# A graph-attention and hypergraph kernel: first two pairs laid out anew, half a weights' sum off TensorE, node degrees of two pairs by one-column products, two leaky heads moved behind an eviction

## The chip, the cores and the metric

One NeuronCore of one Trainium2 chip runs the whole program. The metric is the device time of one execution in microseconds. Three executions of the kernel before took 2388.04, 2384.32 and 2381.41 us; their median, 2384.32 us, is what a change is held against.

## The reference, cut to what matters

There are 128 graphs of 128 nodes with 512 features, and a 128x128 adjacency matrix for each. Layer 0 is graph attention with eight heads, layer 1 a hypergraph network with a hidden width of 1024; each ends in a residual and a layer norm.

```python
# layer 0
feats = einsum('bnf,hfu->bhnu', X, W)                  # 8 heads of 64
dense = leaky_relu(e_self[..., :, None] + e_neigh[..., None, :], 0.2)
att   = softmax(dense + NEG_BIG * (1 - A))
x = layernorm(x + relu(einsum('bhij,bhju->bhiu', att, feats) + b))
# layer 1: H = (adj != 0), w = first row of adj
Dn = einsum('nce,ne->nc', H, w);  Dn = where(Dn > 0, 1/Dn, 0)
Be = H.sum(axis=1);               Be = where(Be > 0, 1/Be, 0)
conv(x, W) = Dn * (H @ (Be * (H.T @ (x @ W.T)))) + b   # used twice
x = layernorm(x + conv(layer_norm(relu(conv(x, W1))), W2) + x)
```

All arithmetic is float32. The biases are zero and the norms' gains one in the data, but the kernel reads them.

## The kernel before, in words

The graphs are taken two at a time, as 64 pairs. The work of a pair runs over about five periods, so that in any one period several pairs are under way, each in another stage ("lag"). The order of the work is written out by hand: every step has a time on a scale with a period of T = 38.6, all steps are sorted by it, and the instructions are issued in that order on the engine that each step names. The numbers are thus keys for an order and no measured times. The dictionary `first` gives single steps of early pairs a key of their own. Each engine takes its instructions strictly in that order, as does the queue of SP, which issues nearly all transfers.

In one period TensorE does, for the pairs then due: `propagate` (tile `pz`: y times the propagator R), `propagator` (`pd`), the hidden layer's chain (`phX`, `phY`, `phW`), `output` (`pq`), the chain of the features (`pfX`, `pfY`, `pfW`), the attention products (`pav`), and the chain of the second layer (`pyX`, `pyY`, `pyW`). Each chain computes a 2x2 blocked product with seven block products instead of eight (a Winograd form). It needs sums of blocks of the data (`zS`, `xS`, `hS`, made by GpSimd, here POOL) and of the weights (made once). In a chain the accumulator `X` is copied out by ScalarE (`ph`, `pf`, `py`, line 359) between two of its products, and the next product into the same bank waits for the copy. PSUM has eight banks, given out in turn.

Steps that the change and the prediction touch:

- `prepare_hidden` (L249) makes sums of W1's blocks on POOL. The sum called s3 is made on TensorE instead, by `prepare_hidden_products` (L263, L264): the identity times one block minus the identity times another, in two halves of 512 columns, each evicted by ScalarE (`prepare_hidden_out`, L267).
- `nodes` (L375 to L384) computes 1/Dn: VectorE multiplies the mask by the first row, which has been spread over all partitions by DMA (`load_first_row`, two transfers of 64 KB), sums along the row, inverts, transposes. `write_nodes` sends it to DRAM, `spread_nodes` brings it back on all partitions as `dnb`. `r_evict` (L468) multiplies `pd` by it.
- Attention scores of a pair come as rows in DRAM (`spread_rows`: DVE `rows`, L559, then the transfer `rd`), are spread to all partitions (`neighbours`: the transfer `nb`), masked on POOL (`masked`, L608, four instructions of four heads), put through leaky ReLU on ScalarE (`leaky`, L624, one instruction for each head, four for each g and q), reduced by VectorE (`largest`, L630), exponentiated on ScalarE (`exponential`, L638), sent to DRAM (`e_write`, `ed`) and read back in blocks (`e_read`, `eb`) for VectorE's 32x32 transpose (`eT`, L659).
- `z_evict` (L866) is ScalarE's copy of `pz`; the first product of the hidden chain waits for it. On ScalarE it stands behind `leaky(0, 0)` and `leaky(0, 1)` of a later pair. `z_sums` (L877) on POOL follow, behind the four mask instructions.
- `relu` (L918), `square` (L929), `y_sum` (L972), `skip` (L842) and `f_sum` (L526) belong to the chains' ends.

Of the kernel before, what the change touches and what calls it, by code (L numbers as in the profile page):

```python
# [8 lines left out]
F32 = mybir.dt.float32  # L9
AF = mybir.ActivationFunctionType  # L10
ALU = mybir.AluOpType
# [9 lines left out]
def kernel(  # L21
# [45 lines left out]
    nc = tc.nc  # L67
    G, N, F = x.shape
    P = 128
# [3 lines left out]
    KF = F // P  # L73
# [3 lines left out]
    HH = H // 2  # L77
# [11 lines left out]
    def bank(name):  # L89
        return psum.tile([P, HALF], F32, tag="bank", name=name)  # L90
# [17 lines left out]
    def load_first_row(p):  # L108
        s = st[p]
        s["w"] = work.tile([P, 2, N], F32, tag="w", name=f"w_{p}", bufs=2)  # L110
        for g in range(2):
            nc.sync.dma_start(s["w"][:, g, :], adj[2 * p + g, 0, :].partition_broadcast(P))
# [92 lines left out]
    ident = const.tile([P, P], F32, name="ident")  # L205
# [52 lines left out]
    def prepare_hidden_banks():  # L258
        made["s3"] = [bank(f"s3_{k}") for k in range(KF // 2)]

    def prepare_hidden_products():
        for k, t in enumerate(made["s3"]):
            nc.tensor.matmul(t, ident, w1_sb[:, 0, k, :], start=True, stop=False)  # L263
            nc.tensor.matmul(t, made["minus"], w1_21[:, k, :], start=False, stop=True)  # L264

    def prepare_hidden_out(k):
        nc.scalar.copy(w1_sb[:, 5, k, :], made["s3"][k])  # L267

# [99 lines left out]
    @step(0, 11.0)  # L368
    def nodes(p, s):

        a = s["a"]
        dd = small.tile([P, 2], F32, tag="dd", name=f"dd_{p}")
        w = s["w"]
        for g in range(2):
            nc.vector.scalar_tensor_tensor(  # L375
                w[:, g, :], a[:, g, :], 0.0, w[:, g, :], op0=ALU.not_equal, op1=ALU.mult,
                accum_out=dd[:, g:g + 1],
            )
        t = dn[:, :2]
        nc.vector.tensor_scalar(t, dd, TINY, None, op0=ALU.max)  # L380
        nc.vector.reciprocal(t, t)
        nc.vector.scalar_tensor_tensor(t, dd, 0.0, t, op0=ALU.is_gt, op1=ALU.mult)
        s["dr"] = work.tile([P, B], F32, tag="dr", name=f"dr_{p}")
        nc.vector.transpose(s["dr"], dn)  # L384

    @step(0, 17.0)
# [224 lines left out]

    def leaky(p, s, g, q):
        if (p, g, q) == (0, 1, 1):

            hs = slice(HH, H)
            t = s["nb"][:, g, HH * N:].rearrange("p (h j) -> p h j", h=HH)
            nc.vector.tensor_tensor(
                t, t, s["ft"][:, g, hs, 0:1].to_broadcast([P, HH, N]), op=ALU.add
            )
            nc.vector.scalar_tensor_tensor(t, t, SLOPE, t, op0=ALU.mult, op1=ALU.max)  # L620
            return
        for h in range(q * HH, (q + 1) * HH):
            t = scores(p, s, g, h)
            nc.scalar.activation(t, t, AF.Prelu, bias=s["ft"][:, g, h, 0:1], alpha=SLOPE)  # L624
# [534 lines left out]
    for t, fn, *args in (  # L1159
# [25 lines left out]
        (78.985, prepare_hidden_banks, ()), (98.05, prepare_hidden_products, ()),  # L1185
        (116.95, prepare_hidden_out, (0,)), (119.86, prepare_hidden_out, (1,)),
        (15.5, prepare_output_vectors, ()), (16.0, prepare_output, ()),
        (78.3, prepare_rows, ()), (78.79, prepare_output_sums, ()),
        (78.99, prepare_output_spread, (0, "gw")), (98.0, prepare_output_spread, (1, "bw")),
        (98.1, prepare_output_bias, ()), (98.2, prepare_output_blocks, (slice(0, 1),)),  # L1190
        (98.25, prepare_output_blocks, (slice(1, 2),)),
# [8 lines left out]

    first = {
        ("square", 0, 0, 1): 134.82,
        ("square", 0, 0, 0): 134.81,
        ("scale_edges", 2): 139.25,
        ("exponential", 1, 1, 0): 126.51,
        ("squares", 0, 1, 2): 144.2,
# [3 lines left out]
        ("first_output", 0, 0): 97.817,  # L1210
        ("write_nodes", 2): 147.1,
        ("nodes", 2): 147.0,
        ("edges", 3): 149.9,
# [5 lines left out]
        
        ("scale_edges", 1): 119.84,  # L1220
        ("edges", 1): 98.5,
        ("exponential", 1, 1, 1): 126.52,
        
        ("exponential", 1, 0, 1): 121.77,
        ("exponential", 1, 0, 0): 119.9,
        ("largest", 1, 1, 1): 121.9,
        ("largest", 1, 1, 0): 119.83,
        ("largest", 1, 0, 1): 117.83,
        ("largest", 1, 0, 0): 98.3,
        ("leaky", 1, 1, 1): 121.8,  # L1230
        ("leaky", 1, 1, 0): 119.82,
# [13 lines left out]
        
        ("propagator", 1): 121.7, ("spread_nodes", 1): 80.3, ("r_evict", 1): 121.8,
        ("leaky", 0, 1, 1): 77.65, ("leaky", 0, 0, 1): 73.6, ("largest", 0, 0, 1): 75.3,
# [13 lines left out]
        
        ("nodes", 3): 154.6, ("write_nodes", 3): 154.7, ("skip", 0): 132.5,
    }
# [4 lines left out]
    for p, time, fn, *args in (  # L1268
# [5 lines left out]
        (1, 15.6, plain_features_out), (1, 97.9, adj_transpose_first),  # L1274
        (0, 78.8, e_transpose_first, 0, 0), (0, 78.85, e_transpose_first, 0, 1),
        (0, 97.815, rstd_first, 0), (0, 97.816, shift_first, 0),
        (0, 97.835, rstd_first, 1), (0, 110.32, shift_first, 1),
# [3 lines left out]
    for p in range(PAIRS):  # L1281
# [4 lines left out]
        for lag, time, name, pairs, fn, args in steps:  # L1286
            if p not in pairs:
                continue
            if p == 0 and lag == 2 and time < 8.5:
                time *= 0.2  # L1290
            if p == LAST:

# [64 lines left out]
```

## Time and profile before

| | |
|---|---|
| three executions | 2388.04, 2384.32, 2381.41 us; median 2384.32 us |
| the profiled execution | 2381.18 us, its span 2379.4 us |
| TensorE busy (matmuls) | 2358.8 us, 99% of the span |
| weight loads, VectorE, POOL, ScalarE busy | 78%, 87%, 77%, 64% |
| granted TensorE clock, mean | 0.999 |
| DMA | 347.09 MB, mean 146 GB/s |

The profile is of one execution; 1.8 us of its time lie outside its span. The page gives busy shares of engines over the whole span. Since one engine is nearly always busy, the time is read from the few places where that engine stands idle. The timeline lists the instructions in order with the idle time ahead of each in square brackets, and what ended it. A start of one group less the start of the group before is the time that the first really takes; the printed durations overlap by some 0.15 us. The waits list who waited for whom in total. PE is TensorE, DVE is VectorE, ACT is ScalarE.

### The profile page before, as it was taken

The page shows a single profiled execution, that of the slowest core. Times are in us where ns is not written, and L with a number is a line of the kernel's source. Part 1 is how long each engine was busy: PE and PEld are TensorE (multiplying, and loading weights), DVE is VectorE, ACT ScalarE, POOL GpSimd, SP SyncE. Part 2 cuts the span into 40 slices and gives each one's busy share as a digit, 9 for nine tenths or more (in the row PEclk, how much of TensorE's full clock was granted, in tenths as well). Part 3 has the DMA queues.
Part 4 walks back from the last instruction along what each step waited for, and adds up shares of the span by engine and source line. Part 5 has one row for each costly group of instructions (what it writes and reads, how often), then busy time and mean ns, then how long its engine had stood idle before and what let it go on. Part 6 is the DMA issues. An engine that isn't in the chain of part 4 may idle for free.

```text
span 2379.4 us, 80693 instructions
## 1 busy us (share of the span) xinstructions
PE 2358.8 (99%) x32317; PEld 1867.3 (78%) x32317; DVE 2077.1 (87%) x4451; ACT 1530.4 (64%) x4489; POOL 1826.4 (77%) x2062
## 2 busy tenths in 40 slices
PE   8999999999999999999999999999999999999998
PEld 6788887887877878778778778788787787787886
DVE  7988988889889898898898898988988988889886
ACT  5676675666766756667667667566676676665663
POOL 5878777787787777877877877778778778787784
PEclk9999999999999999999999999999999999999999
DMA  7555455545544555455555545554555455455431
GB/s 203 142 159 144 141 157 143 151 141 150 151 143 143 155 147 147 146 149 148 150 144 156 143 143 155 150 144 145 149 149 148 147 147 151 141 157 143 146 118 50
DMA packets 431134, 347.09 MB, mean 146 GB/s; under 512 B 151440, under 2 KB 380328, under 8 KB 430760
## 3 DMA queue, kind: packets, MB, share of 16 engines
q1 hardware_dynamic: 427288, 337.46, 49.7%
q8 instruction: 256, 4.19, 0.7%
q10 hardware_dynamic: 3472, 4.47, 0.6%
q14 instruction: 118, 0.97, 0.2%
HBM read 239.08 MB, written 102.73 MB: 144 GB/s over the span
## 4 chain that ended last, share of the span: by engine, by line
PE 93%; DMA 3%; POOL 1%; ACT 1%; DVE 1%; issue 1%; SPq 0%; ACTq 0%; POOLq 0%; DVEq 0%
PE phX L97 18%; PE pyX L97 17%; PE pfX L97 9%; PE phW L97 9%; PE pyW L97 9%; PE pfW L97 4%; PE phY L97 4%; PE pav L724 4%; PE pq L97 4%; PE pz L97 4%; PE pyY L97 4%; PE pfY L97 2%; PE pd L97 1%; DMA nb<-rd 1%; DMA ed<-nb 1%
## 5 line engine op out<-in xcount | busy, mean ns | idle before, releaser
L359 ACT COPY py<-pyX 128x257 f32<-128x257 f32 x189 | 70.6, 374 | 526.4 <-PE pyX L97 458.9
L97 PEld LDWEIGHTS phX<-zS,w_sb 128*64 128x64 f32 x6144 | 345.3, 137 | 35.9 <-POOL ft L763 23.7
L97 PE MATMUL phX<-zS,w_sb 128*64 128x128 f32 x6144 | 368.0, 273 | 0.7 <-POOL xS L486 0.7
L941 POOL TENSOR_TENSOR sq<-sq 128x512 f32<-128x512 f32 (+2 forms) x384 | 343.8, 896 | 20.0
L608 POOL TENSOR_TENSOR nb<-nb,neg 128x512 f32<-128x512 f32 x256 | 319.6, 1282 | 35.2 <-DMA nb<-rd 34.8
L624 ACT ACTIVATE nb<-nb,ft 128x128 f32<-128x128 f32 x1020 | 325.4, 392 | 19.7 <-POOL nb L608 19.5
L638 ACT ACTIVATE nb<-nb,nm 128x128 f32<-128x128 f32 x1024 | 319.1, 392 | 0.2 <-DVE nm L630 0.2
L788 POOL TENSOR_TENSOR rso<-veo,mhalf 128x2 f32<-128x2 f32 x63 | 44.1, 700 | 337.5 <-DVE veo L786 337.5
L918 ACT ACTIVATE h<-h,vecs 128x128 f32<-128x128 f32 x768 | 240.0, 393 | 1.9 <-DVE h L903 1.4
L97 PE MATMUL pyW<-w_sb,hS 128*64 128x256 f32 x2016 | 239.5, 379 | 1.2 <-DVE y L972 1.2
L97 PE MATMUL pyX<-w_sb,h 128*64 128x257 f32 x2016 | 240.1, 379 | 0.5 <-ACT py L359 0.5
L97 PE MATMUL pyX<-w_sb,hS 128*64 128x257 f32 x2016 | 240.2, 379 | 0.1
L630 DVE TENSOR_REDUCE nm<-nb 128x4 f32<-128x512 f32 x256 | 175.2, 684 | 55.9 <-ACT nb L624 45.1
L763 POOL TENSOR_TENSOR ft<-ft,b_bc 128x512 f32<-128x512 f32 x128 | 204.5, 1617 | 5.0 <-ACT ft L550 5.0
L97 PEld LDWEIGHTS pyX<-w_sb,h 128*64 128x64 f32 x2016 | 144.8, 136 | 75.1 <-ACT py L359 0.9
L97 PEld LDWEIGHTS pyW<-w_sb,hS 128*64 128x64 f32 x2016 | 143.9, 136 | 75.7 <-DVE y L972 1.6
L97 PEld LDWEIGHTS pyX<-w_sb,hS 128*64 128x64 f32 x2016 | 138.9, 136 | 65.4 <-POOL hS L486 0.2
L659 DVE STREAM_TRANSPOSE eT<-eb 128x512 f32<-128x512 f32 x252 | 163.4, 685 | 3.3 <-DMA eb<-ed 2.4
L842 DVE SCALAR_TENSOR_TENSOR o<-y,b_bc 128x512 f32<-128x512 f32 x128 | 165.3, 1330 | 0.0
L929 ACT ACTIVATE sq<-h 128x512 f32<-128x512 f32 x256 | 160.7, 629 | 2.1
L1043 DVE SCALAR_TENSOR_TENSOR y<-y,rsh,bw_bc 128x512 f32<-128x512 f32 x126 | 148.3, 1215 | 15.6 <-POOL rsh L1039 15.6
L486 POOL TENSOR_TENSOR hS<-h 128x512 f32<-128x512 f32 x126 | 161.6, 1283 | 0.3 <-ACT h L918 0.3
(187 smaller groups left out, 5544.3 us busy)
## 6 DMA issues: line engine op xcount, KB each, us to landing
nb<-rd SPq DMA_DIRECT2D x127, 512.0 KB, 5.6
ed<-nb SPq DMA_DIRECT2D x126, 512.0 KB, 3.1
eb<-ed SPq DMA_DIRECT2D x504, 128.0 KB, 2.9
x<-in_x_dram SPq DMA_DIRECT2D x64, 512.0 KB, 4.1
out_dram<-o SPq DMA_DIRECT2D x63, 512.0 KB, 3.1
xb<-in_x_dram SPq DMA_DIRECT2D x248, 128.0 KB, 2.9
a<-in_adj_dram SPq DMA_DIRECT2D x64, 128.0 KB
w<-in_adj_dram SPq DMA_DIRECT2D x128, 64.0 KB, 3.9
```

The source lines that it names most:

```text
L97: nc.tensor.matmul(to[rows], lhs[:, rows], rhs, start=start, stop=stop, skip_group_check=True)
L486: engine.tensor_tensor(t[:, i], in0, in1, op=op)
L608: nc.gpsimd.tensor_tensor(t, t, neg[:, :, None, :].to_broadcast([P, NB, HH, B]), op=ALU.add)
L624: nc.scalar.activation(t, t, AF.Prelu, bias=s["ft"][:, g, h, 0:1], alpha=SLOPE)
L630: nc.vector.tensor_reduce(s["nm"][:, g, hs], scores(p, s, g, hs).rearrange("p b h j -> p h b j"), AX.XY, ALU.max, negate=True,)
L638: nc.scalar.activation(t, t, AF.Exp, bias=s["nm"][:, g, h:h + 1])
L659: nc.vector.transpose(s["eT"][:, g, hs, :].rearrange("p h (b i) -> p h b i", b=NB), s["eb", g][:, :, hs, :].rearrange("p b h j -> p h b j"),)
L763: nc.gpsimd.tensor_tensor(t, t, b0_bc.rearrange("p (h u) -> p h u", h=H), op=ALU.add)
L842: nc.vector.scalar_tensor_tensor(s["o"][:, g, :], s["y"][:, g, :], 2.0, b2_bc, op0=ALU.mult, op1=ALU.add)
L918: nc.scalar.activation(dst[:, k, :], src[:, k, :], AF.Relu, bias=b1_sb[:, c:c + 1])
L929: nc.scalar.activation(s["sq"][:, g, q * KH // 2:(q + 1) * KH // 2, :], hid(s, g, q), AF.Square, scale=DH ** -0.5,)
L941: nc.gpsimd.tensor_tensor(t[:, :n, :], t[:, :n, :], t[:, n:2 * n, :], op=ALU.add)
```

## The change

It has four parts.

1. Half of W1's sum s3 stays on TensorE; the other half is made by one POOL instruction, `prepare_hidden_rest`, between the first `z_sums` and `prepare_hidden(3)`.
2. For pairs 2 and 3 the first row is loaded as a column (128 elements of four bytes for each graph), and Dn is a product of the transposed mask with that column on TensorE (`sum_nodes`, tile `pn`, a bank of its own). `nodes` then only inverts and transposes, reading the bank. `sum_nodes(2)` stands ahead of the features' chain of pair 2, and `sum_nodes(3)` between the first two products of pair 1's hidden chain.
3. New keys for pairs 0 to 3: `propagator(1)` goes from ahead of the chain's product 5 to between its products 7 and 4; the copy of `bw` goes behind pair 0's normalized output on ScalarE; `exponential(1, 0, 0)`, `(1, 0, 1)` and `(1, 1, 0)` come earlier, `leaky(1, 1, 1)` later; the first copy of the features' chain goes ahead of `relu(0, 1)` of pair 0; `nodes` and `write_nodes` of pairs 2 and 3 move.
4. For pairs 2 to 24, two of the four heads of `leaky(0, 1)` go from ahead of the two `z_evict` copies to behind them; `largest(0, 1)` goes with them, and `exponential(0, 0)` goes behind the first copy of the hidden chain.

The number of instructions changes little otherwise; from pair 25 on the order is the same as before.

```diff
     def load_first_row(p):
         s = st[p]
+        if p in (2, 3):
+            s["w"] = small.tile([P, 2], F32, tag="wc", name=f"w_{p}", bufs=2)
+            for g in range(2):
+                nc.sync.dma_start(
+                    s["w"][:, g:g + 1], adj[2 * p + g, 0:1, :].rearrange("o e -> e o")
+                )
+            return
...
     def prepare_hidden_products():
-        for k, t in enumerate(made["s3"]):
-            nc.tensor.matmul(t, ident, w1_sb[:, 0, k, :], start=True, stop=False)
-            nc.tensor.matmul(t, made["minus"], w1_21[:, k, :], start=False, stop=True)
+        t = made["s3"]
+        nc.tensor.matmul(t, ident, w1_sb[:, 0, 0, :], start=True, stop=False)
+        nc.tensor.matmul(t, made["minus"], w1_21[:, 0, :], start=False, stop=True)
...
+    def prepare_hidden_rest():
+        nc.gpsimd.tensor_tensor(
+            w1_sb[:, 5, 1, :], w1_sb[:, 0, 1, :], w1_21[:, 1, :], op=ALU.subtract
+        )
...
     def nodes(p, s):
-        a = s["a"]
-        dd = small.tile([P, 2], F32, tag="dd", name=f"dd_{p}")
-        w = s["w"]
-        for g in range(2):
+        if p in (2, 3):
+            dd = s["pn"][:, :2]
+        else:
+            dd = small.tile([P, 2], F32, tag="dd", name=f"dd_{p}")
+        a, w = s["a"], s["w"]
+        for g in range(0 if p in (2, 3) else 2):
             nc.vector.scalar_tensor_tensor(
...
+    def sum_nodes(p, s):
+        s["pn"] = bank(f"pn_{p}")
+        for g in range(2):
+            nc.tensor.matmul(
+                s["pn"][:, g:g + 1], s["hT"][:, g, :], s["w"][:, g:g + 1], start=True, stop=True
+            )
...
-    def leaky(p, s, g, q):
+    def leaky(p, s, g, q, some=slice(0, HH)):
...
-        for h in range(q * HH, (q + 1) * HH):
+        for h in range(q * HH, (q + 1) * HH)[some]:
...
-        (116.95, prepare_hidden_out, (0,)), (119.86, prepare_hidden_out, (1,)),
+        (116.95, prepare_hidden_out, ()), (120.61, prepare_hidden_rest, ()),
...
-        (98.1, prepare_output_bias, ()), (98.2, prepare_output_blocks, (slice(0, 1),)),
+        (110.35, prepare_output_bias, ()), (98.2, prepare_output_blocks, (slice(0, 1),)),
...
     first = {
+        ("relu", 0, 1, 0): 134.805,
+        ("largest", 1, 1, 1): 126.555,
+        ("write_nodes", 2): 130.75,
+        ("nodes", 2): 130.45,
+        ("write_nodes", 3): 156.55,
+        ("nodes", 3): 156.5,
+        ("e_write", 1, 1): 127.4,
+        ("exponential", 1, 1, 1): 127.35,
+        ("leaky", 1, 1, 1): 126.505,
+        ("exponential", 1, 1, 0): 121.79,
+        ("scale_edges", 1): 119.92,
+        ("relu", 0, 0, 1): 133.2,
+        ("r_evict", 1): 127.1,
+        ("propagator", 1): 127.0,
...
-        ("exponential", 1, 1, 0): 126.51,
-        ("write_nodes", 2): 147.1,
-        ("nodes", 2): 147.0,
-        ("scale_edges", 1): 119.84,
-        ("exponential", 1, 1, 1): 126.52,
-        ("largest", 1, 1, 1): 121.9,
-        ("leaky", 1, 1, 1): 121.8,
-        ("propagator", 1): 121.7, ("spread_nodes", 1): 80.3, ("r_evict", 1): 121.8,
+        ("spread_nodes", 1): 80.3, 
-        ("nodes", 3): 154.6, ("write_nodes", 3): 154.7, ("skip", 0): 132.5,
+        ("skip", 0): 132.5,
...
+        (2, 130.3, sum_nodes), (3, 156.41, sum_nodes),
...
+            if 1 < p < 25:
+                late = {
+                    ("leaky", 0, 1): 2.03, ("largest", 0, 1): 2.04, ("exponential", 0, 0): 4.1,
+                }.get((name,) + args)
+                if late is not None:
+                    if name == "leaky":
+                        todo.append((time + (p + lag) * T, run, (fn, p, args + (slice(0, 2),))))
+                        args += (slice(2, 4),)
+                    time = late + (2 - lag) * T
```

More of the change, by code (lines that the diff above doesn't have):

```diff
@@ L258, in prepare_hidden_banks, with prepare_hidden_out @@
     def prepare_hidden_banks():
-        made["s3"] = [bank(f"s3_{k}") for k in range(KF // 2)]
+        made["s3"] = bank("s3")
     def prepare_hidden_products():
-        for k, t in enumerate(made["s3"]):
[L263 to L267, printed above, removed]
+        t = made["s3"]
+        nc.tensor.matmul(t, ident, w1_sb[:, 0, 0, :], start=True, stop=False)
+        nc.tensor.matmul(t, made["minus"], w1_21[:, 0, :], start=False, stop=True)
+    def prepare_hidden_out():
+        nc.scalar.copy(w1_sb[:, 5, 0, :], made["s3"])
+    def prepare_hidden_rest():
+        nc.gpsimd.tensor_tensor(
+            w1_sb[:, 5, 1, :], w1_sb[:, 0, 1, :], w1_21[:, 1, :], op=ALU.subtract
+        )
     def prepare_vectors():
```

## The prediction

> **What bounds the kernel now.** I read the page first, then the waits of TensorE by stretches, then the timeline around each of its idle places.
>
> ```profile
> span 2379.4 us, 80693 instructions
> PE 2358.8 (99%) x32317; PEld 1867.3 (78%) x32317; DVE 2077.1 (87%) x4451; ACT 1530.4 (64%) x4489; POOL 1826.4 (77%) x2062
> PE 93%; DMA 3%; POOL 1%; ACT 1%; DVE 1%; issue 1%; SPq 0%; ACTq 0%; POOLq 0%; DVEq 0%
> ```
>
> TensorE is the bound: 20.6 us of the span are idle, 93% of the chain that ended last is its own. A gain is TensorE work removed or idle time closed. The idle places that the change can reach are these starts in TensorE's timeline:
>
> ```profile
> 45.72 1.02 PE L263 MATMUL s<-w_sb,ident 128*128 128x512 f32 x2
> 46.58 1.02 PE L264 MATMUL s<-w,minus 128*128 128x512 f32 x2
> 47.53 1.97 PE L97 MATMUL pz<-R,y 128*64 128x128 f32 x32
> ...
> 56.79 1.92 PE L97 MATMUL phX<-zS,w_sb 128*64 128x128 f32 x32
> 59.44 1.97 PE L97 MATMUL phX<-zS,w_sb 128*64 128x128 f32 x32 [0.73 <-POOL xS L486]
> ...
> 65.44 1.11 PE L97 MATMUL pfX<-w_sb,xS 128*64 128x264 f32 x8 [0.51 <-ACT pf L359]
> ...
> 83.58 1.95 PE L97 MATMUL pyW<-w_sb,hS 128*64 128x256 f32 x16 [1.18 <-DVE y L972]
> ...
> 124.90 1.97 PE L97 MATMUL phX<-zT,w_sb 128*64 128x128 f32 x32 [0.81 <-ACT zT L866]
> ```
>
> Four waits, each with another owner. From 160 us on a period, from one `pz` to the next, takes 36.37 us when nothing is late. In pairs 3 to 22 it is sometimes longer, as at 779 us, where the order of events on POOL and ScalarE is plain:
>
> ```profile
> 778.05 4.98 POOL L608 TENSOR_TENSOR nb<-nb,neg 128x512 f32<-128x512 f32 x4 [2.46 <-DMA nb<-rd]
> 779.36 1.28 ACT L624 ACTIVATE nb<-nb,ft 128x128 f32<-128x128 f32 x4 [1.84 <-POOL nb L608]
> 780.54 0.35 ACT L970 COPY y<-pyX 128x256 f32<-128x256 f32 x1
> 780.79 1.28 ACT L624 ACTIVATE nb<-nb,ft 128x128 f32<-128x128 f32 x4
> 781.97 1.04 ACT L866 COPY zT<-pz 128x512 f32<-128x512 f32 x2
> 782.59 0.66 PE L97 MATMUL phX<-zT,w_sb 128*64 128x128 f32 x8 [1.06 <-ACT zT L866]
> ```
>
> The transfer `nb` lands late, the mask, eight leaky heads and only then `zT` follow, and TensorE waits. The waits of POOL say where this happens, 165 to 950 us first, then 950 to 2300:
>
> ```profile
> POOL nb L608 <- DMA nb<-rd: 20.4, 20, 2.5
> POOL nb L608 <- DMA nb<-rd: 4.6, 7, 1.3
> ```
>
> Past 950 us a period is 36.37 us throughout, but for one of 36.48; nothing is to be had there.
>
> **The change part by part**, in time against the profiled execution (2381.18 us, of which 1.8 lie outside the span).
>
> *Half of s3.* The second pair of products goes from 45.72 to 47.53: -1.81 us. `pz` can follow: its first y is ready at 44.7, its second at about 46.4. Only ScalarE's `zT` is near, and `bw` is taken from ahead of y. POOL gets one 128x512 subtraction, 1.27 us by row `hS` (L486); the other half is needed by product 7 at about 54.5, and POOL, which idled 1.01 us for `zT` at 50.32, has it by 53.5. The s4 sum behind it ends at 55.8 instead of 55.6, needed at 58.9. Cost on the path: none while POOL keeps that margin of 1 us.
>
> *One-column products.* Each pair adds two products with a full 128x128 weight load, two passes each, so four loads. No row has one column. Nearest is the transpose row `px` (L412): eight in 0.95 us from 14.34 to 15.29, 0.119 each with such a load; four are 0.48 us. The Trainium skill, "TensorE: Matmul & The Clock Gate", sections "Back-to-back issue gap" and "LDWEIGHTS", gives about 25 ns as least issue time however few the columns, and columns over 1.2 GHz for a load, 107 ns; as an estimate, 4 x 132 = 0.53 us. It speaks against the change: the load, not the column, is paid. Bounds 0.2 (loads pulled under other matmuls) and 0.7 (`pt`, 0.18 each); I take 0.48, twice: +0.96. Their inputs are early (hT(2) at about 60.0 for 60.7; hT(3) at 85.4 for 86.7); the banks they take were read long before. On the queue of SP the columns are as many transfers as before, at the same place, loaded tens of us ahead. `write_nodes(2)` now stands ahead of `xb(3)` and would hold it if `dr` came after 66.8; I expect 65.5. `write_nodes(3)` stays ahead of `ed(2, 0)`, with 1 us to spare.
>
> *`pd` moved.* Between product 7 (ends 56.79 + 1.75 = 58.54) and product 4 (59.44) TensorE waits 0.90 us for ScalarE's copy of `phX`, whatever releaser the row names. `pd` (54.61 to 55.04) now fills 0.43: -0.43.
>
> *`pf` copy ahead of the relu.* 63.84 + 0.89 = 64.73 to 65.44: -0.71. The relu behind it has 0.3 us slack to VectorE's next sum.
>
> *`nodes(2)` on VectorE.* Before, it held `y_sum` (80.75 to 83.14), and product 3 started at 83.58 instead of 80.46 + 1.73 = 82.19: -1.39. But its rest now stands at about 63.4 us, ahead of the transposes `eT`, `skip` (2.34 us) and `f_sum`, which TensorE's `pfW` awaits at about 68.3. How long the rest takes:
>
> ```profile
> 81.29 0.46 DVE L380 TENSOR_SCALAR dn<-dd 128x2 f32<-128x2 f32 x1
> 81.98 0.99 DVE L382 SCALAR_TENSOR_TENSOR dn<-dd,dn 128x2 f32<-128x2 f32 x1
> 100.14 0.17 DVE L380 TENSOR_SCALAR dn<-dd 128x2 f32<-128x2 f32 x1
> 100.54 0.16 DVE L382 SCALAR_TENSOR_TENSOR dn<-dd,dn 128x2 f32<-128x2 f32 x1
> ```
>
> Beside POOL's work pair 2 took 1.9 us to the transpose's end, pair 4 0.8. The skill, "SBUF — State Buffer", section "Who interferes with whom", says that a VectorE instruction with two SBUF inputs waits for a GpSimd instruction that reads SBUF, one with a single such input doesn't. The new sums lie in PSUM, so by the rule 0.8 us and no wait (`f_sum` ends at 68.1); by the row of pair 2, 1.9 us and a wait of about 1.1. I take the middle: +0.6, bounds 0 and 1.3.
>
> *What is late next.* With TensorE some 3.3 us earlier at `pz` of pair 1, ScalarE no longer keeps up: its y (81.72 to 83.13) hangs on POOL's `rsa` and VectorE's chain, which start at `xb(3)` and gain only about 0.9 us. Walking it: y ends 82.5, four leaky heads 83.7, the copy 84.0, two heads 84.5, `zT` 85.0; TensorE is ready at 84.3. So +0.7 (0 to 1.2); with all eight heads ahead of it, it would be 1.3.
>
> *Two heads behind `zT`.* A head takes 0.29 us, so `zT` follows a late mask 0.59 us sooner. At pair 2 the period is 37.41, an excess of 1.04; 0.45 stays: -0.6. In pairs 3 to 22 the excess beyond 36.37 that goes with a late `zT` sums, period by period, to 3.06 us (the largest 1.29, 0.69, 0.28, 0.26, 0.23). Less 0.59 each, 0.7 and 0.1 remain: -2.25. POOL's `zS` behind the masks comes next, level with it only at the largest. The moved heads push `exponential(0, 1)` and `ed` back by the same 0.59; the blocks then land by 22.9 us after `pz` at worst, where VectorE reads them at 24.0. VectorE's `largest` moves inside idle time.
>
> Sum: -1.81 + 0.96 - 0.43 - 0.71 - 1.39 + 0.6 + 0.7 - 0.6 - 2.25 = -4.93 us, so 2376.3 for the profiled execution. That one is as fast as the fastest of the three; the median, 2384.32, is 3.14 above it. What differs is not shown. The only waits of varying size are the late transfers, so as an estimate I give the two heads 40% of it (2.25 of 3.06 is 73% of small stalls, 0.59 of 1.29 is 46% of a large one): another -1.3. Median: 2384.32 - 6.2 = 2378.1 us.
>
> **The rivals.**
> *More closes than I count.* The loads of the one-column products hide, neither new wait comes, the varying stalls go wholly: -1.81 + 0.4 - 0.43 - 0.71 - 1.39 - 0.8 - 3.06 - 2 = -9.8, 2374.5 us. For it: each cover exists. Against: VectorE is 87% busy and the margins are tenths.
> *The first periods give it back.* POOL and VectorE have hardly any idle time from 45 to 85 us; a transfer that does not come earlier (`xb(3)`, landing at 73.6) pins `y_sum` and all behind it. Then of the first periods' net 2.1 us nothing is left, and about -2.9 from the heads: 2381.4. For it: the chain of waits runs over exactly these transfers.
> *Slower.* `ed` 0.59 later feeds the ring of transfers `ed`, `eb`, `rd`, `nb`. After pair 1 VectorE already waited 0.55 us for `eb`, and that ring took 37.43 us (`ed` at 91.96 and 129.39). It decides from the point where `ed` to the last `eb` takes 1.2 us more than the slowest period of pairs 3 to 22; then each of 22 periods loses 0.59, +13.0, less 2.1: about 2395. Against: the smallest slack there was 1.8 us, as far as the trace tells landings, and from pair 2 on VectorE never waited for `eb`.
>
> **How the numbers follow.** Forecast 55% (2376 to 2381), more closes 27%, given back 13%, slower 5%. A measurement tells about 0.3%, 7.15 us, from no change, so 2377.2 is the line for faster. It cuts the forecast's case about a third in; with the first rival nearly whole that makes 0.46 faster, 0.49 same, 0.05 slower. The range 2372.5 to 2385.5 leaves out the slower case and the ends of the others, with runs some 2 us apart.
>
> **What would show it.** `pz` of pair 0 at 45.7; product 4 idle 0.4 to 0.5; no idle ahead of `pfX` product 6; `pn` at about 0.5 a pair; `pyW` product 3 some 3 us earlier; a wait at `pfW` for `f_sum`, and a small one for `zT` at pair 1; over pairs 3 to 22 under 1 us of excess. I am wrong if `pz` of pair 3 starts less than 1.5 or more than 4 us earlier than 159.14, or if the periods up to pair 24 show other waits.

## The result and the profile after

The changed kernel takes 2381.25 us (median of 21 runs, 2378.68 to 2383.66), the kernel before, on the same chip, 2384.66 us (21 runs, 2380.15 to 2388.68). The ratio is 0.9985, 95% interval 0.9978 to 0.9992: 3.4 us faster, between 1.9 and 5.2. The forecast was 6.2 us faster; the rival in which the first periods give their gain back stood at 2381.4. A second timing on another chip, told below, gave 0.9992 (0.9985 to 0.9998), with medians 2.4 us apart.

The profiled execution of the changed kernel took 2382.95 us, its span is 2381.2 us. Its page, the head and the shares of the chain that ended last:

```profile
span 2381.2 us, 80693 instructions
PE 2359.2 (99%) x32321; PEld 1940.1 (81%) x32321; DVE 2075.2 (87%) x4443; ACT 1532.2 (64%) x4488; POOL 1829.8 (77%) x2063
...
PE 92%; DMA 3%; POOL 2%; ACT 1%; DVE 1%; issue 1%; SPq 0%; POOLq 0%; DVEq 0%; ACTq 0%
```

TensorE is the bound as before: 2359.2 us busy, 22.0 us of the span idle. This span is 1.8 us longer than the profiled one of before, although the median is 3.4 us shorter: one profile of either kernel does not show the gain. The reason became clear only with more profiles, and it is the main lesson of this case.

TensorE's timeline of the changed kernel at the places that the prediction named (start, duration, group, idle time ahead of it and its releaser):

```profile
46.02 1.09 PE L97 MATMUL pz<-R,y 128*64 128x128 f32 x16 [0.75 <-DVE R L491]
47.40 1.09 PE L97 MATMUL pz<-R,y 128*64 128x128 f32 x16 [0.29 <-ACT y L854]
...
58.08 1.97 PE L97 MATMUL phX<-zS,w_sb 128*64 128x128 f32 x32 [0.25 <-ACT ph L372]
...
61.73 0.60 PE L405 MATMUL pn<-w,hT 128*128 128x1 f32 x4
...
70.22 1.11 PE L97 MATMUL pfW<-w_sb,xS 128*64 128x264 f32 x8 [0.48 <-DVE ft L549]
...
81.67 1.93 PE L97 MATMUL pyW<-w_sb,hS 128*64 128x256 f32 x16
83.40 1.95 PE L97 MATMUL pz<-R,y 128*64 128x128 f32 x32
...
86.22 1.97 PE L97 MATMUL phX<-zT,w_sb 128*64 128x128 f32 x32 [0.43 <-ACT zT L889]
88.12 0.61 PE L405 MATMUL pn<-w,hT 128*128 128x1 f32 x4
...
122.02 1.95 PE L97 MATMUL pz<-R,y 128*64 128x128 f32 x32
```

Read it beside the rows of before. The second pair of `s` products is gone, but `pz` now waits for R and for y. Product 4 (58.08) waits 0.25 us instead of 0.73, the second `pfX` and product 3 of `pyW` (81.67) have lost their old waits, `pfW` has a new one for `ft`, and the first `phX` of pair 1 a new one for `zT`. The period from 83.40 to 122.02 takes 38.62 us, where it took 36.37 before. `pz` of pair 3 starts at 158.39, only 0.75 us earlier than before.

The late transfers go on past pair 24. Waits of POOL's mask, 165 to 950 us and 950 to 2300 us (total us, count, median us), in the changed kernel:

```profile
POOL nb L631 <- DMA nb<-rd: 24.4, 21, 2.5
POOL nb L631 <- DMA nb<-rd: 13.4, 14, 2.4
```

The second row was 4.6 us before. The heads that stand ahead of `zT` belong to the pair behind that of `pz`, so the last period with moved heads is that of pair 23. At pair 26, where the order of the instructions is that of before, the old pattern stands whole, from the rows of POOL, ScalarE and TensorE: late `nb`, mask, eight heads, then `zT`:

```profile
997.61 4.97 POOL L631 TENSOR_TENSOR nb<-nb,neg 128x512 f32<-128x512 f32 x4 [2.40 <-DMA nb<-rd]
998.92 1.28 ACT L647 ACTIVATE nb<-nb,ft 128x128 f32<-128x128 f32 x4 [1.79 <-POOL nb L631]
1000.36 1.28 ACT L647 ACTIVATE nb<-nb,ft 128x128 f32<-128x128 f32 x4
1001.54 1.05 ACT L889 COPY zT<-pz 128x512 f32<-128x512 f32 x2
1002.16 1.97 PE L97 MATMUL phX<-zT,w_sb 128*64 128x128 f32 x32 [1.19 <-ACT zT L889]
```

### The profile page after: what moved, and what is told of

Read it like the earlier page. It is cut to its first block, busy times and chain, and to the rows that moved or that the text cites. A ratio compares the mean times of both kernels' runs of the same rounds, so it can differ in the third digit from the quotient of the medians.

```text
span 2381.2 us, 80693 instructions
## 1 busy us (share of the span) xinstructions
PE 2359.2 (99%) x32321; PEld 1940.1 (81%) x32321; DVE 2075.2 (87%) x4443; ACT 1532.2 (64%) x4488; POOL 1829.8 (77%) x2063
## 4 chain that ended last, share of the span: by engine, by line
PE 92%; DMA 3%; POOL 2%; ACT 1%; DVE 1%; issue 1%; SPq 0%; POOLq 0%; DVEq 0%; ACTq 0%
PE phX L97 18%; PE pyX L97 16%; PE pfX L97 9%; PE phW L97 9%; PE pyW L97 8%; PE pfW L97 5%; PE phY L97 5%; PE pq L97 4%; PE pav L747 4%; PE pz L97 4%; PE pyY L97 4%; PE pfY L97 2%; DMA nb<-rd 2%; PE pd L97 1%; DMA rd<-rows 1%
## 5 line engine op out<-in xcount | busy, mean ns | idle before, releaser
L97 PEld LDWEIGHTS pyX<-w_sb,h 128*64 128x64 f32 x2016 | 158.4, 136 | 61.5 <-ACT py L372 0.9
L97 PEld LDWEIGHTS pyW<-w_sb,hS 128*64 128x64 f32 x2016 | 158.6, 136 | 59.6
L97 PEld LDWEIGHTS pyX<-w_sb,hS 128*64 128x64 f32 x2016 | 152.3, 136 | 52.9 <-POOL hS L509 0.2
```

Of the source, the lines that this page charges most:

```text
L97: nc.tensor.matmul(to[rows], lhs[:, rows], rhs, start=start, stop=stop, skip_group_check=True)
```

## The experiments

Two theories were set against each other. A: the moved heads carry the result, about 3 us, and the new first periods net about nothing. B: the first periods carry it. Below, "excess" is what the periods of a stretch of pairs take beyond 36.37 us each, summed from the starts of `pz`; "new order" is the layout of the first periods with both pairs of columns.

### The heads, undone, alone, and for all pairs

```diff
 # heads undone, in the changed kernel
-            if 1 < p < 25:
+            if 1 < p < 2:
 # heads alone: the same block with "1 < p < 25" put into the kernel before
 # heads for all: in the changed kernel
-            if 1 < p < 25:
+            if 1 < p < 60:
```

> The change without its fourth part (all four heads of leaky(0, 1) ahead of zT again, largest and exponential in their old places); the rest as in the changed kernel. Theory A (the first two periods give back most of what they gained, at waits for R, y, f_sum and zT; the moved heads carry the result): 0.3 to 1.3 us faster than before, and in the trace a wait for zT at pair 1 of about 1.0 instead of 0.43 us. Theory B (the new layout of the first periods carries the result, the heads little): 2.5 to 3.5 us faster than before.

> The kernel before with the fourth part alone. Theory A: 2 to 3.3 us faster than before; late-zT excess in pairs 3 to 22 under 1 us where before it was 3.1, and a few tenths at pair 2. Theory B: within 0.7 us of before, the stalls as long as before because the mask arrives later by what the heads were moved.

> The changed kernel with the heads moved for pairs 2 to 59 instead of 2 to 24. Theory A with stalls that go on past pair 24 (0.7 to 1.4 us each at pairs 24, 26 and 28 of the changed kernel's profile, where transfers were still slow): 1 to 2 us faster than the changed kernel, about 4.5 to 5.5 faster than before, and no excess over 0.8 us in any period after pair 24. If the moved heads cost something where transfers are quick: equal to the changed kernel or slower by up to 1 us, and periods longer than 36.37 us past pair 32.

All three against the kernel before at 2382.33 us on that chip. Heads undone: 2382.43 us, ratio 1.0001 (0.9993 to 1.0009). Heads alone: 2379.27 us, 0.9986 (0.9979 to 0.9992). Heads for pairs 2 to 59: 2378.43 us, 0.9984 (0.9976 to 0.9991). So the heads alone give about what the change gives, and the other three parts together nothing that can be measured (the interval leaves 1.7 us faster to 2.1 slower): A holds, B falls. Without the heads, TensorE waits 1.21 us at pair 1 from start to start (1.01 shown as idle), where the prediction had 1.3 for all eight heads ahead of `zT`:

```profile
86.78 1.97 PE L97 MATMUL phX<-zT,w_sb 128*64 128x128 f32 x32 [1.01 <-ACT zT L889]
```

The twelve runs gave fourteen profiles with those of the two kernels, from several chips. The excess of pairs 3 to 23, the periods in which heads are moved, was 2.68, 3.26, 3.84 and 4.30 us in the four without moved heads, and 0.20, 0.36, 0.37, 0.48, 0.59, 1.06, 1.15, 1.31, 2.14 and 2.61 us in the ten with them. The middles are 3.6 and 0.8 us, 2.7 us apart, which is near what the times say. The first profile of the changed kernel is the 2.61: the most disturbed of the ten. Moved heads do not close every such wait: with the heads for pairs 2 to 59 one period, that of pair 36, was still 0.92 us too long at `zT`, where none over 0.8 was expected.

### Half of s3 alone

```diff
 # in the kernel before
...
-            nc.tensor.matmul(t, ident, w1_sb[:, 0, k, :], start=True, stop=False)
-            nc.tensor.matmul(t, made["minus"], w1_21[:, k, :], start=False, stop=True)
+        nc.tensor.matmul(t, ident, w1_sb[:, 0, 0, :], start=True, stop=False)
+        nc.tensor.matmul(t, made["minus"], w1_21[:, 0, :], start=False, stop=True)
...
+    def prepare_hidden_rest():
+        nc.gpsimd.tensor_tensor(w1_sb[:, 5, 1, :], w1_sb[:, 0, 1, :], w1_21[:, 1, :], op=ALU.subtract)
```

> The kernel before with part 1 alone: half of s3 off TensorE, made by POOL. The prediction's term is -1.81 us at the first pz, so the first phX at 47.5 instead of 49.33 (first transposes at the same instant). The rival, read from the changed kernel's trace, is that pz is then bound by R (VectorE) and by the second y (ScalarE), as there (idle 0.75 and 0.29): the first phX at 48.1 to 48.6, a gain of 0.7 to 1.2. In both cases pz of pair 3 shows whether it survives: 157.4 to 158.4 if all later waits move along, 159.1 if a wait further on (product 4 for ph, pyW for y_sum) takes it back.

TensorE's timeline of this kernel:

```profile
45.87 2.21 PE L97 MATMUL pz<-R,y 128*64 128x128 f32 x32
47.91 1.95 PE L97 MATMUL phX<-zT,w_sb 128*64 128x128 f32 x32
...
82.19 1.95 PE L97 MATMUL pyW<-w_sb,hS 128*64 128x256 f32 x16 [1.23 <-DVE y L977]
83.97 1.92 PE L97 MATMUL pz<-R,y 128*64 128x128 f32 x32
```

`pz` comes 1.66 us earlier, and with nothing to wait for; the first `phX` 1.42 us, between what the two theories had put; `pz` of pair 3 starts at 158.15, 0.99 us earlier. The one time, 2380.67, stands on the 2380.66 of the kernel before; with a spread of 7 us among single runs it says nothing by itself. The term of the prediction was thus right in this execution. But here, as in the profile of before, TensorE's granted clock was at half for 3.4 us just ahead of `pz` (see the last section), and that made it late enough for R. In the two profiles of the old order without the half clock, R is done only 0.65 and 1.01 us ahead of the start of `pz`, so a gain of 1.81 could not have come whole. In the first profile of the changed kernel, also without it, the first `phX` starts at 48.36, a gain of 0.97, and `pz` waits for R.

### The columns, undone and alone

```diff
 # undone, in the changed kernel: pairs 2 and 3 as all others
-        (2, 130.3, sum_nodes), (3, 156.41, sum_nodes),
-        ("nodes", 2): 130.45,
+        ("nodes", 2): 147.0,
-        ("nodes", 3): 156.5,
+        ("nodes", 3): 154.6,
 # alone: load_first_row, nodes, sum_nodes and these keys put into the kernel before
```

> The changed kernel with part 2 undone: nodes of pairs 2 and 3 are again wide sums on VectorE (rows spread by DMA, old keys), the other parts stay. It sizes the one-column products together with what they move. By the prediction's terms: no pn (-1.06 us as measured at 61.73 and 88.12), no wait of pfW for f_sum (-0.6), no wait for zT at pair 1 (-0.6), but pyW product 3 waits again by about 1.2 to 1.4 for y_sum; pz of pair 3 about 157.3 to 157.8 instead of 158.39, so the time 0.6 to 1 us under the changed kernel's, 2380 beside a before of 2382.3 to 2384.7. The rival, that the columns pay because the wide sums hold more than y_sum (scale_edges, the hidden chain's sums): pyW waits by 2 us or more, pz of pair 3 at 159.5 or later, and the time 1 to 2 us above the changed kernel's.

> The kernel before with part 2 alone: the degrees of pairs 2 and 3 by one-column products, with the keys of nodes and write_nodes as in the changed kernel. By the prediction's terms alone it would give -1.39 (no wait of product 3 for y_sum) +0.96 (columns) +0.6 (pfW for f_sum), so pz of pair 3 within 0.5 us of 159.14. The stretch in which nb is issued 2.7 us or more after rd ended at pair 23 in the kernel before, at pair 25 with the heads moved, at pair 16 in the changed kernel without its columns, and at pair 31 in three profiles of the changed kernel. If the columns lengthen it, it ends here at pair 28 to 34, with 1 us or more of excess past pair 23 on average, and the time is 0.5 to 2 us over the kernel before. If it goes with the order of the first periods as a whole, it ends at pair 20 to 26, and the time is within 0.7 us.

Without the columns: 2377.59 us beside 2380.66, ratio 0.9987 (0.9980 to 0.9994). Columns alone: 2382.48 beside 2383.05, 1.0 (0.9991 to 1.0008). So the columns as a whole are worth nothing measurable, in either surrounding. In the profiles they do much, but in opposite directions. Without them, in the changed kernel, TensorE waits here:

```profile
46.66 1.09 PE L97 MATMUL pz<-R,y 128*64 128x128 f32 x16 [1.60 <-DVE R L481]
...
70.86 1.11 PE L97 MATMUL pfW<-w_sb,xS 128*64 128x264 f32 x8 [1.18 <-DVE ft L539]
...
83.45 1.95 PE L97 MATMUL pyW<-w_sb,hS 128*64 128x256 f32 x16 [0.94 <-DVE y L985]
```

Product 3 of `pyW` waits again, as expected, but `pfW` still waits for `f_sum`, and longer. That wait is not the columns' doing. `pz` of pair 3 starts at 158.97, where 157.3 to 157.8 was expected. Alone, on the other hand, the columns bring `pz` of pair 3 to 156.95 from 159.14, and then lose it: the excess of pairs 3 to 61 is 4.45 us. Much of the 2.19 us is not theirs: that profile has no half-speed clock, and neither has that of the heads for all pairs alone, where the old order of the first periods has `pz` of pair 3 at 157.57.

### The round trip in the period from pair 1 to pair 2

That period took 38.62 us in the first profile. VectorE's timeline there; first the changed kernel, then its second profile, then the kernel before:

```profile
83.14 0.21 DVE L1015 STREAM_TRANSPOSE sr<-sums_in 128x32 f32<-128x32 f32 x1
...
89.83 0.45 DVE L1033 STREAM_TRANSPOSE so<-sums_out 128x256 f32<-128x256 f32 x1 [2.18 <-DMA sums_out<-sd]
...
90.39 1.27 DVE L653 TENSOR_REDUCE nm<-nb 128x4 f32<-128x512 f32 x2
```

```profile
82.97 0.21 DVE L1015 STREAM_TRANSPOSE sr<-sums_in 128x32 f32<-128x32 f32 x1
...
88.56 0.45 DVE L1033 STREAM_TRANSPOSE so<-sums_out 128x256 f32<-128x256 f32 x1 [1.07 <-DMA sums_out<-sd]
```

```profile
84.36 0.21 DVE L992 STREAM_TRANSPOSE sr<-sums_in 128x32 f32<-128x32 f32 x1
...
87.79 0.68 DVE L630 TENSOR_REDUCE nm<-nb 128x4 f32<-128x512 f32 x1
...
90.54 0.40 DVE L1010 STREAM_TRANSPOSE so<-sums_out 128x256 f32<-128x256 f32 x1
```

VectorE writes row sums (`sr`) that go to DRAM and come back spread (`sums_out`), and `so` reads them. From the end of `sr` to the start of `so` it took 6.48, 5.38 and 5.97 us. Before, the wide sums of pair 3 and a reduction filled that time, and `so` waited for nothing. In the changed kernel both stand elsewhere, and VectorE idles while `nm` is queued behind `so`; ScalarE's exponential then waits 1.04 us for `nm`. The next experiment puts `so` behind `nm` and `nodes(3)`, a second one adds wide sums of pair 3 at their old place and heads for all pairs, and the changed kernel itself ran twice more, once a single time and once timed in full.

```diff
 # so late, in the changed kernel
-    @step(4, 1.7, until=LAST - 1)
+    @step(4, 2.2, until=LAST - 1)
     def sum_rest(p, s):
 # combined: this, and
-        if p in (2, 3):
+        if p == 2:
-            if 1 < p < 25:
+            if 1 < p < 60:
 # the changed kernel again, once (e2_again) and timed (e3_whole): no edit
```

> The changed kernel once more, unchanged, for a second profile of it. If the stretch of late transfers (nb issued 2.7 to 3.2 us after rd instead of 1.4) lasts to pair 30 because of the new first periods, it ends there again, within two pairs, and pairs 25 to 61 show 1.5 us of excess or more. If its end differs from execution to execution, it ends elsewhere, say at pair 20 to 26, and pairs 25 to 61 show under 0.7 us. The first periods repeat to 0.1 us in both cases: pz of pair 3 at 158.4, product 4 idle 0.25, zT idle 0.43 at pair 1.

> The changed kernel itself, timed beside the two others on one chip, and a third profile of it: about 2.5 to 3.5 us under the kernel before. In the profile the period from pz 1 to pz 2 follows the wait of so: about 36.55 plus the columns' 0.53 and zT's 0.6 where so waits about 1.1 us, and 0.4 us more for each further 0.5 us of that wait; the excess of pairs 3 to 61 anything between 0.6 and 6 us.

> The changed kernel with one step moved: VectorE's transpose so (sum_rest), which reads the transfer sums_out, goes behind the two nm reductions and, for pair 0, behind nodes(3), instead of ahead of them. In the changed kernel so waited 2.18 us (1.07 in the second profile) for that round trip through DRAM (from the end of sr to the start of so 6.5 and 5.4 us), with nm, dn and all later VectorE work queued behind it, ScalarE's exponential idle 1.04 us for nm, and the period from pz of pair 1 to pz of pair 2 took 38.62 and 37.73 us. If this wait is where the first periods' gain went, so waits under 0.3 us, exponential does not idle, that period takes 37.3 to 37.6, pz of pair 3 starts at 156.9 to 157.4, and the time is 0.5 to 1.5 us under the changed kernel's. If the round trip is paid in any case, because rsh and y behind it keep VectorE's later work where it was, the period stays at 37.7 to 38.6 and the time within 0.4 us. Later so might also hold rsh on POOL (needed at 90.6): then y starts later than 92.9 and the period exceeds 38.6.

> The changed kernel with three edits: the so step moved as in the kernel before this one, the two heads moved for pairs 2 to 59, and nodes of pair 3 as wide sums on VectorE again at their old place ahead of so, where VectorE waited for the round trip (so no second pn, -0.53 us on TensorE). If the first periods' gain was lost to that wait, the period from pz 1 to pz 2 takes 36.9 to 37.2, pz of pair 3 starts at 156.4 to 157.0, and the median is 1.5 to 2.5 us under the changed kernel's, so about 4.5 to 6 under the kernel before. If the waits merely move on to the next transfer, it stays within 0.7 us of the changed kernel.

Beside 2381.01 us of the kernel before: the changed kernel 2378.65, ratio 0.9992 (0.9985 to 0.9998); `so` late 2378.33, 0.9989 (0.9982 to 0.9995); combined 2377.91, 0.9986 (0.9979 to 0.9992). The single run took 2377.72. In the second and third profile of the changed kernel the period was 37.73 and 37.70 us, `pz` of pair 3 at 157.35 and 157.09. With `so` late:

```profile
89.19 0.40 DVE L1033 STREAM_TRANSPOSE so<-sums_out 128x256 f32<-128x256 f32 x1
...
91.37 2.35 DVE L1066 SCALAR_TENSOR_TENSOR y<-y,rsh,bw_bc 128x512 f32<-128x512 f32 x2 [0.56 <-POOL rsh L1062]
```

`so` no longer waits, and the period is 37.72 all the same: my theory, that this wait costs the first periods' gain, falls for an ordinary execution. A wait of 1.1 us at `so` is not on the path; the period is 37.7 there because of `pn` (0.53), `zT` (0.64 from start to start) and 0.16 at starts of groups. With a wait of 2.18 us, in the first profile, it was 38.62, and the rows show where the 0.9 us more came from. ScalarE first, then TensorE:

```profile
95.76 1.28 ACT L661 ACTIVATE nb<-nb,nm 128x128 f32<-128x128 f32 x4 [0.42 <-DVE nm L653]
96.95 0.56 ACT L372 COPY ph<-phX 128x512 f32<-128x512 f32 x1
...
99.65 1.28 ACT L941 ACTIVATE h<-h,vecs 128x128 f32<-128x128 f32 x4 [0.95 <-DVE h L926]
...
103.03 0.36 ACT L372 COPY pf<-pfX 128x264 f32<-128x264 f32 x1
```

```profile
97.66 1.97 PE L97 MATMUL phX<-zS,w_sb 128*64 128x128 f32 x32
99.67 1.97 PE L97 MATMUL phW<-zT,w_sb 128*64 128x128 f32 x32
...
103.54 1.11 PE L97 MATMUL pfX<-w_sb,xS 128*64 128x264 f32 x8
```

VectorE, late by its wait at `so`, has `nm` late for ScalarE's exponential; the copy of `phX` stands behind that, and TensorE's next product behind the copy; VectorE's `h` and ScalarE's copy of `pf` follow. From start to start the three products lose 0.25, 0.27 and 0.29 us against the second profile, 0.86 with a start of a group. So a long round trip does reach TensorE, by these rows; no run forces one. With the heads undone the period was 38.49 at a wait of only 0.73, but there `zT` costs 1.21 us instead of 0.64, and the same `pfX` another 0.15. In the combined kernel the wide sums of pair 3 pushed `so` to 90.45, y to 92.52, and the period to 38.78, at least 1.6 us over what I had expected. Its median is 0.74 us under that of the changed kernel, with intervals that overlap: it is not shown to be better.

### Where the late transfers end

In the first part of every profile `nb` is issued about 3 us after `rd`, because SP's queue waits for `rd` to reach DRAM; later the same wait is 1.4 us. SP's queue at one and the same time, first in the changed kernel, then in the kernel before:

```profile
987.36 0.33 SPq L592 DMA_DIRECT2D rd<-rows  x1
990.51 0.92 SPq L612 DMA_DIRECT2D nb<-rd  x2
```

```profile
987.65 0.33 SPq L569 DMA_DIRECT2D rd<-rows  x1
989.07 1.27 SPq L589 DMA_DIRECT2D nb<-rd  x2
```

From 3.15 to 1.42 us; after that switch a period is 36.37 us with few exceptions. The switch is not sharp: single quick ones come before it, single waits of 2.2 to 2.7 us after it. Counting the quick stretch from the pair behind the last wait of 2.8 us or more, it began at pair 22 in the kernel before, 25 with the heads alone, and 31, 29 and 29 in the three profiles of the changed kernel. (The expectations count single later waits in and so name 23 and three times 31.) So it goes mainly with the program and less with the execution. Two more runs look at it.

```diff
 # heads for all pairs in the kernel before
-            if 1 < p < 25:
+            if 1 < p < 60:
 # the changed kernel without its columns, and the column transfers issued in addition
+        if p in (2, 3):
+            wc = small.tile([P, 2], F32, tag="wc", name=f"wc_{p}", bufs=2)
+            for g in range(2):
+                nc.sync.dma_start(wc[:, g:g + 1], adj[2 * p + g, 0:1, :].rearrange("o e -> e o"))
```

> The kernel before with only the heads moved, for pairs 2 to 59 instead of 2 to 24. If the moved heads carry the result and late transfers occur past pair 24 in most executions, it is 0.3 to 1.5 us under the kernel with heads moved to pair 24 (2379.3), so 2378 to 2379, and 3.5 to 4.5 under the kernel before; pairs 25 to 61 show under 0.7 us of excess. If pairs past 24 have no stalls unless the first periods are laid out anew, it equals that kernel within 0.3 us: 2379 to 2379.6. If moving the heads where nothing is late costs (ed 0.6 later each period), it is slower than 2379.6.

> The changed kernel with wide nodes for pairs 2 and 3 (its late stretch ended at pair 16), and the four column transfers of the first rows issued in addition, their data unused. If these transfers of 128 single elements are what lengthens the stretch, it ends near pair 31 as in the changed kernel. If not (then it is the order of work, or the place of the transfers among the others), it ends near pair 16, or elsewhere without a pattern. The first periods stay as in the kernel with wide nodes: R waited for by pz 0 up to 1.6 us, pyW product 3 waiting 0.9, pz of pair 3 at 158.5 to 159.2, plus up to 1 us if the transfers delay others on SP's queue.

Heads for all pairs alone: 2378.17 us beside 2380.66, ratio 0.9989 (0.9982 to 0.9995), the quick stretch from pair 25, and no excess from pair 24 on; so moving the heads past pair 24 without the new first periods has nothing to win, and no cost shows. With the column transfers in addition the quick stretch began at pair 16, exactly as without them; the single run took 2377.14 us.

| kernels | quick stretch from pair | excess of pairs 24 to 61, us |
|---|---|---|
| old order: before, heads alone, s3 alone, heads for all alone | 22, 25, 19, 25 | 0.11, 0.03, 0.00, 0.00 |
| changed, without columns; the same with extra transfers | 16, 16 | -0.01, -0.13 |
| changed (three profiles) | 31, 29, 29 | 3.23, 1.01, 0.52 |
| heads undone, so late, heads for all in the new order | 29, 29, 36 | 1.62, 0.68, 1.39 |
| old order with columns alone | 33 | 1.77 |
| combined (one pair of columns) | 32 (26 but for a single late one) | 0.19 |

The five programs with both pairs of columns have the quick stretch from pair 29 to 36, the one with one pair from 32, the six without from 16 to 25; the columns' transfers as such do not make the difference. What of the columns does it (the bank that each takes in the turn of eight, the place of `write_nodes` in SP's queue, the shift of the order) was not taken apart, and why the switch happens at all stays open.

## Why the prediction was right or wrong

It gave 2378.1, with a range of 2372.5 to 2385.5; measured 2381.25, 3.4 us faster than the kernel before instead of 6.2. The total lies in the range, and the heads did what was forecast; that the range holds it owes something to luck, since the first periods, which were to give 2.1 us net, gave nothing that the run without the heads could measure. By the forecast's own sign of being wrong, `pz` of pair 3 less than 1.5 us earlier, the first profile is wrong with 0.75; the second and third have 1.79 and 2.05. The other sign came too: product 4 of the hidden chain waited 0.45 us at pair 8, and from pair 24 on there was excess. The rival "the first periods give it back" came nearest, but by another way than it said.

*Half of s3, -1.81.* Right where nothing else is late: 1.66 us at `pz` in the kernel with this part alone. The step that failed is "`pz` can follow", which looked at y alone: in the changed kernel it waits 0.75 us for R and 0.29 for the second y. The profile that the step was read from had TensorE at half clock there, which hid R. The gain at the first `phX` is 0.97.

*One-column products, 0.48 each.* Measured 0.53 from start to start, both times (61.73 to 62.26, 88.12 to 88.65). The row of `px` gave 0.48; the estimate from the Trainium skill, "TensorE: Matmul & The Clock Gate", sections "Back-to-back issue gap" and "LDWEIGHTS", 0.53. The page was the better guide: what is paid is the weight load, however few the columns.

*`pd` moved, -0.43, and the `pf` copy first, -0.71.* Both as said: product 4 still starts 0.42 us later than the 0.43 us of `pd` ahead of it need, and product 6 of `pfX` has no idle time ahead.

*The rest of `nodes(2)` and `pfW`, +0.6.* The size was right (0.70 from start to start), the cause wrong. VectorE's timeline in the changed kernel:

```profile
63.83 0.15 DVE L395 TENSOR_SCALAR dn<-pn 128x2 f32<-128x2 f32 x1
64.01 0.17 DVE L396 RECIPROCAL dn<-dn 128x2 f32<-128x2 f32 x1
64.21 0.16 DVE L397 SCALAR_TENSOR_TENSOR dn<-pn,dn 128x2 f32<-128x2 f32 x1
...
65.81 3.92 DVE L865 SCALAR_TENSOR_TENSOR o<-y,b_bc 128x512 f32<-128x512 f32 x2
69.66 0.42 DVE L549 TENSOR_TENSOR ft<-pf,pfW 128x264 f32<-128x264 f32 x1
```

From PSUM the small instructions took 0.15 to 0.17 us each and the chain, with its transpose, 0.8, which agrees with the rule of the page "SBUF — State Buffer", section "Who interferes with whom"; pair 2 had taken 1.9 before. (The page gives its rule for one SBUF input only outside VectorE's two-port modes; the forecast left that out, and of its own rows a one-input instruction took 0.46 us beside POOL and 0.17 without; in which mode is not shown.) The time went into `skip`, two instructions that I had carried over at the 2.34 us of before and that took 3.92 here, 3.94 with s3 alone and 3.28 with the heads for all alone. It reads two operands from SBUF. Before, it started at 66.28, when POOL's sum of 128x1024 elements (62.86 to 66.22) was just over; here it started at 65.81, beside that sum:

```profile
65.12 2.37 POOL L234 TENSOR_TENSOR w_sb<-w_sb 128x1024 f32<-128x1024 f32 x1
```

Where `skip` starts while that sum runs, it is longer by nearly what is left of the sum: 0.47, 1.04, 1.68 and 2.16 us were left with the columns alone, with the heads for all alone, here and without the columns, and `skip` took 2.71, 3.28, 3.92 and 4.40. That goes with the longer wait of `pfW` without the columns. (With s3 alone `skip` starts ahead of the sum, and both are slowed.) A duration is a row of its surroundings; moved, it has to be costed anew, by the same rule that I applied only to the new instructions.

*`pyW` product 3, -1.39.* The wait is gone, but it had not been a fixed cost: with the heads for all alone, with the same keys for pairs 0 and 1, it was 0.19 us. There VectorE's `eT` waited 0.46 us for `eb` instead of 1.37 (first that kernel, then the kernel before), which I take to be why:

```profile
69.82 1.30 DVE L659 STREAM_TRANSPOSE eT<-eb 128x512 f32<-128x512 f32 x2 [0.46 <-DMA eb<-ed]
```

```profile
70.98 1.30 DVE L659 STREAM_TRANSPOSE eT<-eb 128x512 f32<-128x512 f32 x2 [1.37 <-DMA eb<-ed]
```

*`zT` at pair 1, +0.7.* Measured 0.64 from start to start (0.43 shown as idle). With the second columns that makes the period 37.5, and three of the four profiles that share the order up to there had 37.70 to 37.73; the first had 0.9 more, by the late round trip.

*`zT` at pair 2, -0.6.* It came as -1.04, the period is 36.37; but it is so with the heads undone as well, and with the columns alone. With the heads alone it is 36.37 too, but the period ahead of it grew by 0.87 us. I read it so that TensorE, held up by the columns in the period before, no longer comes ahead of `zT`; no run takes that apart. The step credited to the heads a wait that also goes without them.

*The heads in pairs 3 to 24, -2.25.* Right in mechanism and size: 0.8 us of excess were to remain, and 0.8 is the middle of ten profiles, with 0.2 to 2.6 in single ones. The further 1.3 for the median was built on the profile of before being an undisturbed one. It was not: its 3.26 us lie among the 2.7 to 4.3 of the four profiles without moved heads. In time the heads alone gave 3.1 us, where their terms with pair 2 came to 4.15.

*What no step had.* I had written that from pair 25 on the order is the same and nothing is to be had there. The same order does not mean the same time: the late stretch ends seven to nine pairs later, and in most of these periods the eight heads are again ahead of `zT`. From pair 24 on the three profiles of the changed kernel lost 3.23, 1.01 and 0.52 us, the six kernels without columns 0.1 at most. The eight heads are not all of it, as the 1.39 us with the heads moved for all pairs show.

The sum closes only roughly. Heads -2.7 and late stretch +1.0 leave -1.7 us. The first periods add -0.75 to -2.05 by `pz` of pair 3, if the kernel before is taken with its half clock; against the old order without it (157.57) they add between +0.82 and -0.48. So -0.9 to -3.8 us, against -3.4 and -2.4 measured: profiles of single executions do not tell more closely what the first periods are worth, and the run without the heads tells it to no better than 2 us.

## What to carry to other kernels

Before a gain of a few tenths is read from one profile, sort the waits into those that repeat and those that hang on a transfer, and take a second profile: here 21 executions of the changed kernel on one chip lay between 2376.66 and 2383.15 us, twice the whole change apart. When an instruction is moved, its duration is not moved with it: ask what runs on the engine that shares its memory at the new place. And work taken off a busy engine only pays if what is queued behind it was waiting for that work; where the next thing in the queue is a transfer's return, the engine stands idle instead.

## What the runs showed of the hardware

The granted clock of TensorE fell to half for 3.4 us somewhere between 42 and 47.4 us in eight of the fourteen profiles, always for the same length, and in the other six not at all; the three profiles of the changed kernel have both. The stretch from 42.1 to 45.5 us (length; busy time and instructions of PE, PEld, DVE, ACT, POOL; granted clock; DMA share; GB/s), first in the kernel before, then in the kernel with heads for all pairs alone, whose order is the same there:

```profile
42.10:45.50 3.40, 3.40 (x5) 1.51 (x5) 3.23 (x9) 3.18 (x10) 1.39 (x3) 0.51 1.20 146
```

```profile
42.10:45.50 3.40, 3.40 (x9) 1.41 (x9) 3.12 (x12) 2.02 (x7) 1.73 (x2) 1.00 1.03 167
```

Five products went through in the one, nine in the other. In the old order `pz` then starts 39.8 us after the first transpose with the half clock (before, heads alone) and 38.8 and 38.0 without it; in the changed kernel 37.6 and 37.9 with it and 38.0 without, where R is waited for. What sets the half clock off is not shown. I had not expected that a part of the start differs by a us from one execution to the next for this reason.

The other surprise was the switch of the transfers: from the issue of the write `rd` (at most 128x32 elements) to that of the transfer that waits for it took 3.15 us, and 1.42 us from a pair on that goes mainly with the program, 16 to 36 here, while the order of the transfers in a period stayed the same.
